# Normalization at the end of a fused convolution kernel: scale and shift in one ScalarE operation, max and sum on VectorE, and the parts in another order

## The chip, the core and the metric

The kernel runs on one core of a Trainium2 chip. A core has TensorE (PE in the profile) for matrix products, VectorE (DVE) and GpSimd (POOL) for elementwise work, ScalarE (ACT) for activations, and SyncE (SP), which here only issues transfers. Each engine works through its own instructions in order and waits for others by semaphores. Transfers run on sixteen DMA engines, whichever engine issued them. On-chip memory (SBUF) has 128 partitions; the profile writes a tile as partitions x elements.

The metric is the device time of one execution in microseconds (us), median over runs, lower is better. One further execution is taken by the hardware profiler; its instruction times, counted from the start of its span, are what the views of the profile show.

## The reference, cut to what matters

Four layers follow one another on x of 8 images, 128 channels, 64 x 64 pixels, all in float32. The change concerns only the end of the fourth and the residual sum that follows each layer: the fourth layer samples its input at learned offsets, convolves, normalizes each channel over all images and pixels, applies a leaky ReLU, and is added to the layer's input.

```python
out = jnp.einsum('bckhw,ock->bohw', samp, dcn_w.reshape(COUT, C, KK))
out = out + dcn_b[None, :, None, None]
mu = out.mean(axis=(0, 2, 3), keepdims=True)
var = out.var(axis=(0, 2, 3), keepdims=True)
out = (out - mu) * lax.rsqrt(var + 1e-05)
out = out * gamma[None, :, None, None] + beta[None, :, None, None]
return jnp.where(out >= 0, out, 0.1 * out)
```

The kernel's output is x3 plus this result, where x3 is what the first three layers have left. The mean and variance need every image, so nothing can be normalized before the last convolution is done.

## The kernel before, in words

`conv_preact_kernel` (line 35) runs layer 0, then layers 1 to 3 interleaved by a hand-made schedule, and at its very end calls `finish` (lines 1280 to 1323), which holds the whole change. Channels lie on the 128 partitions.

While layer 3 runs, `Layer3.store` (line 1266) takes the statistics of each block of 512 pixels into `st` and writes the convolution's output of the first six images to the DRAM tensor `od`. For the last two images, `KEEP = 2`, the outputs stay in SBUF (`o_kept`), and `Layer2.keep` (line 1131) has fetched the matching pieces of x3 into SBUF too (`x3k`). These are 16 small parts of 128x512: two images of eight blocks. The six other images are 24 large parts of 128x1024 (`E = 2 * T`), whose x3 and `od` pieces must be loaded. They go through `room`, the SBUF tensor X that layer 3 has used as its buffer for gathered samples. It holds eight large parts (`AHEAD = 8`), each a pair of 512 KB pieces.

`finish` works like this. SP issues the loads of the first eight large parts (line 1299), each as soon as layer 3 has left that piece of X. DVE aggregates the statistics (line 1304) and, with ACT's square root (line 1306), makes the per-channel factor `sc` (lines 1307 and 1308). Then one loop runs over the 40 parts: first the 16 small ones, then the 24 large ones. Its iteration n starts part n and ends part n - 1:

- for part n, DVE subtracts the mean and multiplies by `sc` (line 1315), and ACT adds beta (line 1316);
- for part n - 1, DVE takes the max of v and 0.1 v (line 1319), GpSimd adds v to x3 (line 1320), and ACT issues the store of the sum (line 1321). After a large part, SP issues the loads of the large part eight further on, into the same place.

This text order is the order in each engine's queue. So ACT's queue reads: activation of part n, store of part n - 1, activation of part n + 1. A store's issue waits for the sum that it stores, and what stands behind it in ACT's queue waits with it. SP's queue holds only the loads, in order; a load of x3 waits for the store that frees its place to land, and the following load of `od` stands behind it. The small parts have no loads in this stage.

Of the kernel before, what the change touches and what calls it, by code (L numbers as in the profile page):

```python
# [10 lines left out]
F32 = mybir.dt.float32  # L11
I32 = mybir.dt.int32
AF = mybir.ActivationFunctionType
ALU = mybir.AluOpType
# [3 lines left out]
P = 128  # L18
# [5 lines left out]
T = 512  # L24
# [10 lines left out]
def conv_preact_kernel(ctx: ExitStack, tc: tile.TileContext, a: dict, out: bass.AP):  # L35
# [46 lines left out]
    with tc.tile_pool(name="l2w", bufs=1) as wp, tc.tile_pool(name="l2", bufs=2) as w2, tc.tile_pool(  # L82
# [64 lines left out]
        while three.late:  # L147
            three.tick()
        finish(tc, a, eps, od, x3d, y_out, st, const, kept, three.kept, X.rearrange("p n b -> p (n b)"))


# [1128 lines left out]
def finish(tc, a, eps, od, x3d, y_out, st, wp, x3k, odk, room):  # L1280

    nc = tc.nc
    E, AHEAD = 2 * T, 8
    gamma = wp.tile([P, 1], F32, name="gamma")
    nc.sync.dma_start(gamma, a["gamma"])
    beta = wp.tile([P, 1], F32, name="beta")
    nc.sync.dma_start(beta, a["beta"])
    todo = [(b, g) for b in range(B) if (b, 0) not in odk for g in range(HW // E)]

    def place(n):  # L1290

        at = n % AHEAD * 2 * E
        return room[:, at : at + E], room[:, at + E : at + 2 * E]

    def loads(n):
        if n < len(todo):
            b, g = todo[n]
            for t, d in zip(place(n), (x3d, od)):
                nc.sync.dma_start(t, d[b][:, g * E : (g + 1) * E])

    for n in range(AHEAD):
        loads(n)
    mv = wp.tile([P, 2], F32, name="bn_mv")
    nc.vector.bn_aggr(mv, st.rearrange("p a s -> p (a s)"))
    sc = wp.tile([P, 1], F32, name="bn_sc")
    nc.scalar.activation(sc, mv[:, 1:2], AF.Sqrt, bias=eps)
    nc.vector.reciprocal(sc, sc)
    nc.vector.tensor_mul(sc, sc, gamma)

    parts = [(x3k[b, g], odk[b, g], y_out[b][:, g * T : (g + 1) * T]) for b, g in odk]  # L1310
    parts += [(*place(n), y_out[b][:, g * E : (g + 1) * E]) for n, (b, g) in enumerate(todo)]
    for n in range(len(parts) + 1):
        if n < len(parts):
            _, v, _ = parts[n]
            nc.vector.tensor_scalar(v, v, mv[:, 0:1], sc, ALU.subtract, ALU.mult)
            nc.scalar.activation(v, v, AF.Identity, bias=beta)
        if n:
            x3, v, out = parts[n - 1]
            nc.vector.scalar_tensor_tensor(v, v, 0.1, v, ALU.mult, ALU.max)
            nc.gpsimd.tensor_add(x3, x3, v)  # L1320
            nc.scalar.dma_start(out, x3)
            if n > len(odk):
                loads(n - 1 - len(odk) + AHEAD)


def layouts(i):
# [55 lines left out]
```

## Time and profile before

The runs took 7391.58, 7405.77 and 7413.39 us, median 7405.77.

| what | value |
|---|---|
| profiled execution, its own time | 7432.59 us |
| its span, first to last instruction | 7430.9 us |
| busy over the span: PE, DVE, ACT, POOL | 76%, 65%, 45%, 55% |
| factor `sc` ready, first operation of the loop (line 1315) | 7292.56 us |
| last sum on POOL (line 1320) ends | 7423.65 us |
| DVE max, 128x1024 (line 1319), 24 times | 3279 ns mean |
| DVE max, 128x512, 16 times | 1478 ns mean |
| DVE scale and subtract (line 1315), 128x1024 and 128x512 | 801 and 536 ns mean |
| ACT add beta (line 1316), 128x1024 and 128x512 | 1149 and 721 ns mean |
| POOL sum (line 1320), 128x1024 and 128x512 | 2785 and 1528 ns mean |

The engines' shares are means over the whole span, in which other stages have other limits; the stage of `finish` is read from its own stretch. In the order of time a line gives the start, the length, the engine, the source line, the operation with output and inputs, and in brackets how long the engine sat idle before it and what ended that. In the view of stretches the columns are the stretch, its length, busy time with the number of instructions of PE, PEld (weight loads), DVE, ACT and POOL, the granted TensorE clock, the mean busy share of the DMA engines, and GB/s. In the view of waits a line gives who waited for whom, the us in total, how many times, and the longest.

### The profile page before, as it was taken

How to read it: one execution, taken by the hardware profiler on the slowest of the kernel's cores; microseconds unless marked ns; L12 is line 12 of the kernel's file. 1: busy time of each engine (PE TensorE's matmuls, PEld its weight loads, DVE VectorE, ACT ScalarE, POOL GpSimd, SP SyncE). 2: the span in 40 equal slices, each digit the busy share in tenths (PEclk: the TensorE clock that was granted, in tenths of full speed). 3: DMA queues.
4: the chain of work that ended last, by engine and by line, in shares of the span. 5: the costliest groups of instructions: out<-in, count | busy, mean ns of one | idle time of the engine just before them, and what ended most of it. 6: DMA issues, size and time to landing. Idle time of an engine off the chain costs nothing.

```text
span 7430.9 us, 79727 instructions
## 1 busy us (share of the span) xinstructions
PE 5644.5 (76%) x25130; PEld 3377.1 (45%) x25130; DVE 4854.7 (65%) x6350; ACT 3346.5 (45%) x7618; POOL 4120.3 (55%) x3781
## 2 busy tenths in 40 slices
PE   6888888899999999779898988984646555565431
PEld 1222222255556556647777767762333333333220
DVE  4988889666666666230366666758767676676668
ACT  3555655433333332020255555554556555655553
POOL 4878778545545454000255555555666666666665
PEclk9888888799999999989999999996768777776665
DMA  1111111101100100130356656667666666666666
GB/s 57 43 58 54 57 56 53 42 29 34 32 30 30 31 20 18 55 128 24 98 176 194 185 183 180 193 184 246 209 214 214 210 207 207 207 204 220 181 181 245
DMA packets 358982, 926.70 MB, mean 125 GB/s; under 512 B 64040, under 2 KB 99120, under 8 KB 356512
## 3 DMA queue, kind: packets, MB, share of 16 engines
q0 software_dynamic: 184320, 604.13, 26.7%
q1 hardware_dynamic: 168480, 300.70, 12.5%
q10 hardware_dynamic: 5760, 16.78, 0.6%
q8 instruction: 200, 3.28, 0.2%
q14 instruction: 222, 1.82, 0.1%
HBM read 800.16 MB, written 121.21 MB: 124 GB/s over the span
## 4 chain that ended last, share of the span: by engine, by line
PE 55%; ACT 13%; issue 9%; DVE 8%; another core or an unknown queue 8%; POOL 4%; DMA 3%; SPq 0%; DVEq 0%; POOLq 0%; ACTq 0%
PE u_ps L743 13%; PE ps_l L743 11%; ACT X L1203 7%; PE u_ps L579 5%; PE ps_o L1246 4%; PE ps_c L488 3%; PE ps_t L904 3%; PE ps_y L633 3%; PE ps_s L1228 2%; PE ps_x L396 2%; DVE hb L614 2%; PE ps_off L1021 2%; POOL hb L625 2%; PE ps_t L930 1%
## 5 line engine op out<-in xcount | busy, mean ns | idle before, releaser
L1192 POOL DMA_INDIRECT X<-table,idx x1386 | 1315.0, 949 | 743.0 <-issue 277.7
L1192 POOL DMA_INDIRECT got<-table,idx x918 | 881.8, 961 | 1294.0 <-DVE idx L1082 528.8
L625 POOL TENSOR_TENSOR hb<-hb,bc 128x1024 f32<-128x1024 f32 x512 | 1206.2, 2356 | 47.1 <-POOL carry L620 4.5
L614 DVE TENSOR_TENSOR_SCAN hb<-da,carry,u_ps 128x512 f32<-128x512 f32 x896 | 1098.1, 1267 | 76.3 <-PE ps_y L633 19.8
L596 ACT ACTIVATE da<-dt_ps 128x1024 f32<-128x1024 f32 x512 | 524.4, 1024 | 1284.7 <-PE dt_ps L579 1088.0
L1246 PE MATMUL ps_o<-samp,dcn_w 128*128 128x256 f32 x2304 | 716.9, 458 | 221.6 <-issue 90.0
L1203 ACT ACTIVATE X<-X,wgt 128x128 f32<-128x128 f32 x2772 | 865.6, 397 | 24.4 <-issue 24.2
L1238 ACT COPY samp<-ps_s 128x384 f32<-128x384 f32 x768 | 362.6, 472 | 1056.9 <-remote 595.5
L579 PE MATMUL u_ps<-u,m_u 32*128 32x512 f32 x2048 | 653.2, 717 | 130.9 <-DVE hb L614 130.3
L603 DVE TENSOR_TENSOR u_ps<-u_ps,bc 128x1024 f32<-128x1024 f32 x512 | 625.9, 1223 | 191.2 <-PE dt_ps L579 173.9
L1228 PE MATMUL ps_s<-ident,X 128*128 128x128 f32 x1386 | 310.7, 347 | 568.5 <-ACT samp L1238 274.3
L579 PE MATMUL dt_ps<-dt,m_dt 32*128 32x512 f32 x2048 | 665.1, 729 | 31.5 <-ACT da L596 25.7
L1246 PEld LDWEIGHTS ps_o<-samp,dcn_w 128*128 128x128 f32 x2304 | 510.3, 233 | 348.8 <-issue 121.0
L1219 DVE TENSOR_TENSOR prod<-prod,X 128x384 f32<-128x384 f32 x462 | 260.8, 565 | 491.4 <-ACT X L1203 308.9
L751 DVE SCALAR_TENSOR_TENSOR X<-ps_l,X 128x256 f32<-128x256 f32 x252 | 106.7, 423 | 727.0 <-PE ps_l L743 514.1
L1203 ACT ACTIVATE got<-got,wgt 128x128 f32<-128x128 f32 x1836 | 570.3, 393 | 0.7 <-issue 0.7
L1228 PEld LDWEIGHTS ps_s<-ident,X 128*128 128x128 f32 x1386 | 208.6, 178 | 704.1 <-ACT samp L1238 336.1
L620 POOL COPY carry<-hb 128x2 f32<-128x2 f32 x512 | 110.6, 216 | 735.8 <-DVE hb L614 686.5
L1208 DVE TENSOR_TENSOR prod<-X,prod 128x768 f32<-128x768 f32 x462 | 444.3, 962 | 57.4 <-ACT prod L1175 38.3
L751 DVE SCALAR_TENSOR_TENSOR X<-u_ps,X 128x256 f32<-128x256 f32 x252 | 107.0, 425 | 562.9 <-PE u_ps L743 560.5
L904 PE MATMUL ps_t<-xn,w 128*128 128x512 f32 (+4 forms) x688 | 346.1, 658 | 69.7 <-issue 28.0
L579 PEld LDWEIGHTS u_ps<-u,m_u 32*128 32x128 f32 x2048 | 169.8, 202 | 483.8 <-DVE hb L614 281.6
(233 smaller groups left out, 10687.3 us busy)
## 6 DMA issues: line engine op xcount, KB each, us to landing
bc<-bcd SPq DMA_DIRECT2D x512, 64.0 KB
table<-tok SPq DMA_DIRECT2D x128, 256.0 KB
x<-x1d SPq DMA_DIRECT2D x96, 256.0 KB
X<-table,idx POOLq DMA_INDIRECT x1386
x<-x2d SPq DMA_DIRECT2D x48, 384.0 KB
x3h<-x3d SPq DMA_DIRECT2D x16, 1056.0 KB
x_st<-in_x SPq DMA_DIRECT2D x64, 256.0 KB
x_o<-in_x SPq DMA_DIRECT2D x64, 256.0 KB
```

The costliest lines, as they stand in the source:

```text
L579: nc.tensor.matmul(ps[:, j, :], lhsT=mask[q, r].rearrange("p d n -> p (d n)"), rhs=S[c][src, h][q, :], start=True, stop=True,)
L596: nc.scalar.activation(da, steps[i]["dt"], AF.Exp)
L603: nc.vector.tensor_mul(st["bc"], st["bc"], s["bc", h][:, 0].unsqueeze(1).to_broadcast([P, 2, T]))
L614: nc.vector.tensor_tensor_scan(hb[:, j, :], st["da"][:, j, :], st["bc"][:, j, :], start, ALU.mult, ALU.add)
L625: nc.gpsimd.tensor_mul(hb, hb, S[c]["bc", h][:, 1].unsqueeze(1).to_broadcast([P, 2, T]))
L743: nc.tensor.matmul(ps[:, c0:c1, :], lhsT=w[:, k, :], rhs=v[:, prev, c0 + k - PAD : c1 + k - PAD, :], start=(k == PAD), stop=(k == K - 1),)
L904: nc.tensor.matmul(ps[:, o0 - a0 : o1 - a0, :], lhsT=self.w1[:, k, :], rhs=S["xn", g][:, i0 + o0 : i0 + o1, :], start=(k == 2), stop=(k == 4),
L1192: nc.gpsimd.indirect_dma_start(out=got[:, k, :, :].rearrange("p q c -> p (q c)"), out_offset=None, in_=tab, in_offset=bass.IndirectOffsetO ...
L1203: nc.scalar.activation(got[:, k, q, :], got[:, k, q, :], AF.Identity, scale=wgt[:, t, k0 + k, q : q + 1])
L1208: nc.vector.tensor_mul(prod, got[:, :, 0:2, :], w.unsqueeze(3).to_broadcast([P, G3, 2, C]))
L1228: nc.tensor.transpose(ps[:, k, :], got[:, k, 0, :], self.ident)
L1246: nc.tensor.matmul(ps, lhsT=self.dcn_w[:, k, :], rhs=samp[:, k - k0, :], start=(k == 0), stop=(k == KK - 1))
```

## The change

The shift is folded: the kernel makes, once, a per-channel `bn_shift` = beta - mean x sc from two small DVE operations. With it ACT does scale and shift in one activation per part, reading the untouched v, and DVE's operation of line 1315 is gone. DVE does the max as before and then also the sum with x3; GpSimd does nothing in this stage. And the order of the parts is another one: three large parts, two small ones, and so on, eight times, where before all small parts came first. The reload of a large part still follows that part's predecessor in its place; only the counter is kept differently. SP's instructions and their order are the same as before.

```diff
     nc.vector.reciprocal(sc, sc)
     nc.vector.tensor_mul(sc, sc, gamma)
 
-    parts = [(x3k[b, g], odk[b, g], y_out[b][:, g * T : (g + 1) * T]) for b, g in odk]
-    parts += [(*place(n), y_out[b][:, g * E : (g + 1) * E]) for n, (b, g) in enumerate(todo)]
+    shift = wp.tile([P, 1], F32, name="bn_shift")
+    nc.vector.scalar_tensor_tensor(shift, mv[:, 0:1], sc, beta, ALU.mult, ALU.subtract)
+    nc.vector.tensor_scalar_mul(shift, shift, -1.0)
+
+    here = [(x3k[b, g], odk[b, g], y_out[b][:, g * T : (g + 1) * T]) for b, g in odk]
+    parts = []
+    for n, (b, g) in enumerate(todo):
+        parts.append((*place(n), y_out[b][:, g * E : (g + 1) * E]))
+        if n % 3 == 2:
+            parts += [here.pop(0) for _ in range(2) if here]
+    parts += here
+    m = AHEAD
     for n in range(len(parts) + 1):
         if n < len(parts):
             _, v, _ = parts[n]
-            nc.vector.tensor_scalar(v, v, mv[:, 0:1], sc, ALU.subtract, ALU.mult)
-            nc.scalar.activation(v, v, AF.Identity, bias=beta)
+            nc.scalar.activation(v, v, AF.Identity, bias=shift, scale=sc)
         if n:
             x3, v, out = parts[n - 1]
             nc.vector.scalar_tensor_tensor(v, v, 0.1, v, ALU.mult, ALU.max)
-            nc.gpsimd.tensor_add(x3, x3, v)
+            nc.vector.tensor_add(x3, x3, v)
             nc.scalar.dma_start(out, x3)
-            if n > len(odk):
-                loads(n - 1 - len(odk) + AHEAD)
+            if x3.shape[-1] == E:
+                loads(m)
+                m += 1
```

## The prediction

> **What bounds the kernel now.** I read three views of the profiled execution: the stretches of the end stage, then its order of time, then its waits. The change lies wholly behind the last convolution, so only the last 139 us of 7430.9 count.
>
> The first view is busy time by stretch: length, busy us of PE, PEld, DVE, ACT and POOL with instruction counts, granted clock, DMA share, GB/s.
>
> ```profile
> 7300.00:7324.00 24.00, 0.00 (x0) 0.00 (x0) 22.18 (x23) 7.94 (x11) 16.90 (x12) 0.50 0.32 121
> 7324.00:7340.00 16.00, 0.00 (x0) 0.00 (x0) 15.68 (x11) 5.32 (x5) 11.29 (x5) 0.50 0.43 148
> 7340.00:7356.00 16.00, 0.00 (x0) 0.00 (x0) 16.00 (x9) 4.59 (x4) 11.19 (x5) 0.50 0.86 297
> 7356.00:7402.00 46.00, 0.00 (x0) 0.00 (x0) 46.00 (x24) 13.58 (x12) 32.05 (x13) 0.50 1.01 395
> ```
>
> DVE looks full all along. The DMA engines do little for the first 40 us, while the sixteen small parts go through, and are full (395 GB/s) only later. Is DVE's fullness work? The order of time (start, length, engine, line) answers:
>
> ```profile
> 7293.90 0.69 DVE L1319 SCALAR_TENSOR_TENSOR o_kept<-o_kept 128x512 f32<-128x512 f32 x1 [0.33 <-ACT o_kept L1316]
> ...
> 7361.62 0.80 DVE L1315 TENSOR_SCALAR X<-X,bn_mv,bn_sc 128x1024 f32<-128x1024 f32 x1
> 7361.78 2.84 POOL L1320 TENSOR_TENSOR X<-X 128x1024 f32<-128x1024 f32 x1 [1.16 <-DVE X L1319]
> 7362.35 3.36 DVE L1319 SCALAR_TENSOR_TENSOR X<-X 128x1024 f32<-128x1024 f32 x1
> ...
> 7365.62 0.80 DVE L1315 TENSOR_SCALAR X<-X,bn_mv,bn_sc 128x1024 f32<-128x1024 f32 x1
> ```
>
> The first max (512 elements), with GpSimd still idle, took 0.69. A later one of 1024 took 3.36: GpSimd's add ends at 7361.78 + 2.84 = 7364.62 and the max at 7362.35 + 3.36 = 7365.71, only 1.09 later. So the max stood still until the add was over. The add in turn lasts 2.84 here but 2.34 in the last part, where no L1315 runs beside it. DVE and GpSimd take turns: 2.34 add, 1.1 max, some 0.5 scale-and-subtract. The period from L1315 to L1315 is 7365.62 - 7361.62 = 4.00 for a large part; for a small one the starts stand 2.13 apart. Sum 24 x 4.00 + 16 x 2.13 = 130.1; in the trace, from 7292.56 to the last add's end at 7423.65, it is 131.1. The waits show who is held:
>
> ```profile
> ACT X L1316 <- POOL X L1320: 62.8, 22, 2.9
> POOL X L1320 <- DVE X L1319: 25.8, 22, 1.2
> ACT o_kept L1316 <- POOL x3k L1320: 20.4, 14, 2.1
> ```
>
> ACT waits for the adds, since the store's issue (L1321) stands in its queue; DVE hardly waits for anybody on record.
>
> **What the Trainium skill says.** "SBUF — State Buffer", section "Who interferes with whom": a DVE instruction with two SBUF inputs, or in a 2-port mode, and a GpSimd one share a port pair as an exclusive lock, and the second blocks fully. The 1.09 above agrees. "VectorE: DVE Perf Modes", section on the TRN2 errata: an fp32 add of two tensors takes (N+151)/0.96 ns, so 0.69 for 512 and 1.22 for 1024. The trace agrees at 512: 0.686 at L949, an add with one input from PSUM. "ScalarE: Activation LUTs", section "What ACT_TABLE_LOAD costs": each pointer operand of an activation adds about 93 ns. No row here has dense data and two pointers. "DMA: Bandwidth & Descriptors", section "Issuing engines are not separate DMA queues": transfers from ACT and SP share the same 16 engines; the 1.01 share while both queues work agrees.
>
> **The change, part by part.** All times below are those of the profiled execution.
>
> Setup: bn_shift costs two 128x1 DVE operations; L768 shows 0.22 and L1308 0.16 for such, some 0.45 with gaps. The 0.54 of L1315 ahead of the first activation goes. First activation near 7293.1, as before (7293.14). Worth zero within 0.3.
>
> L1315 goes (24 x 0.80, 16 x 0.54), and the activation takes scale as a second pointer: 1.15 + 0.09 = 1.24 large, 0.72 + 0.09 = 0.81 small (estimate from the page). From below it costs nothing more. From above, L721, the only row with both pointers, takes 1.305 for 512, but its output is strided over four batches; I don't take it. Cover: ACT then has 24 x 1.24 + 16 x 0.81 = 42.7, plus 40 issues at 0.34 (13.5), against 83 on DVE.
>
> GpSimd's adds go to DVE, and the lock goes. DVE per large part: max 1.22 + add 1.22 + two gaps of 0.03 (L947 starts 0.78 after L945, which lasts 0.75) = 2.50. The max at 1024 is 0.69 plus 512/0.96 ns. Small: 0.69 + 0.69 + 0.06 = 1.44. Sum 24 x 2.50 + 16 x 1.44 = 83.0, against 130.1.
>
> ACT's queue is ordered activation n, store n-1, activation n+1. The store's issue waits for add n-1; behind it stands activation n+1, and max n+1 waits for that. From the end of add n-1: 0.38 issue with semaphores + 1.24 = 1.62, while DVE does part n, 2.50 or 1.44. Only where n is a second small part and a large one follows does DVE wait, some 0.2, seven times: 1.5.
>
> Interleaving: three large, two small, eight times. Nothing moves on SP's queue; each reload (two transfers of 0.524 MB) still waits for the store of its buffer, eight large parts back. But it is asked for earlier: the first large store goes out near 7297, not 7332.6. Traffic behind 7297: 16 reloads x 1.049 = 16.8 MB and stores 24 x 0.524 + 16 x 0.262 = 16.8 MB, 33.6 in all. DVE alone would ask for 5.24 MB (3 x 0.524 + 2 x 0.262 stored, 3 x 1.049 loaded) in each 3 x 2.50 + 2 x 1.44 = 10.4 us: 504 GB/s, over the 395 of the full stretch (its full slices show 410 and more). So once the eight parts in hand are used up, **transfers set the pace**: they are what is late next.
>
> The sum: the initial loads end near 7297 (in the trace the rate falls to 121 GB/s by 7300), so the flow starts at 7298. When the last load lands, all but some 1.6 MB of stores has moved: 32.0 MB / 0.395 = 81.0, so 7379, and with about 1 for the landing 7380. Then the last large part, 1.2 + 2.5, and two small ones, 2.9: 7386.6. From the last add's end to the span's end it was 7430.9 - 7423.65 = 7.25; with a store of half the size (0.65 less at 395 GB/s) 6.6. Span 7393.2: **38 us less**. At 410 GB/s it is 41 less. Below 395, 2 KB rows of the small stores may cost: their 0.32 share at 121 GB/s means 378 when full, which on 4.2 MB adds 0.5.
>
> The profiled execution took 7432.6, 27 above the median of the runs (7405.8, runs 7391.6 to 7413.4); the end stage is not where I can see that, so I take the 38 off the median: **7368 us**.
>
> **The rivals.** *Vector alone sets the pace* (transfers keep up): first max 7294.4 + 83.0 + 1.5 + 6.6 = 7385.5, 45 less, 7361. For it: 8 parts in hand at the start. Against: 504 GB/s asked, where the highest slice of the transfers' view (7340 to 7402) has 423.
>
> *Transfers come slower than 395*, since reloads wait for stores and a store's issue can stand behind an activation waiting for a load: at 340 GB/s the last load lands at 7393, span 7406.5, 24 less, 7381. For it: stores under full traffic took up to 9.9 us from issue to the reload (7344.64 to 7354.49), and 7340 to 7356 ran at 297 with DVE never idle. Against: there, reloads had only begun.
>
> *Slower: the ring of eight buffers starves.* One round trip (store, reload, compute) would have to exceed 8 x 5.2 us, which is (7423.65 - 7298)/24 per large part; then break-even is 32.0 MB in some 118 us, 270 GB/s, and a clear loss (22 us) needs 228. At 225 the last load lands near 7441: span 7454, 23 more, 7429. For it: the stretch before the end ran at 191 GB/s (7240 to 7270), but on gathers. Against: 46 us at 395 in the same ring.
>
> *The max stays slow without GpSimd*, so the change doesn't do what it says: 24 x (3.36 + 1.25) + 16 x 2.2 = 146, 16 more, 7422. The 0.69 at 7293.90 speaks against it.
>
> **How the numbers follow.** The forecast (gain 34 to 43) has 0.80, vector alone 0.05, slower transfers 0.10, the starving ring 0.03, the slow max 0.02. What a measurement can tell from no change is about 0.3%, 22 us. The forecast's own range is 7363 to 7372, widened by the scatter of a median (runs lie 22 apart) to 7352 to 7384. With vector alone's 7361 less scatter, and slower transfers' 7381 with some, the range is 7347 to 7388. Faster: 0.80 + 0.05, less a little for scatter, plus half of slower transfers, 0.87; within 0.3%: the rest of these and the slow max, 0.10; slower 0.03.
>
> **What would show it.** Right: from the first max on, 1.22 and 0.69 for max and add; no POOL busy in the end stage; DVE full until some 30 to 50 us in, then idle time put down to ACT's activations, and those waiting for loads; DMA share near 1 from about 7300 to 7380; last large part's activation close behind the last load. Wrong: DMA share well under 0.9 with DVE idle (the ring), activations over 2 us, or a max that keeps 3 us.

## The result, and the profile after

The changed kernel takes 7360.31 us (median of 6 runs, 7352.98 to 7377.2), the kernel before 7401.13 us in the same comparison (6 runs, 7391.58 to 7413.39). The ratio is 0.9947 with a 95% interval of 0.9933 to 0.9962: 28 to 50 us less, by the medians 40.8.

The profiled executions differ by more, 7430.9 - 7375.5 = 55.4 us of span, and not all of it is owed to the change. I cut both spans at the same two places: where `sc` is ready (line 1308), and where the last sum ends. I call the stretch between them the loop and what follows it the tail.

| | before | after | difference |
|---|---|---|---|
| ahead of the loop | 7292.5 | 7272.3 | 20.2 |
| loop, 40 parts | 131.1 | 100.1 | 31.0 |
| tail | 7.25 | 3.1 | 4.15 |
| span | 7430.9 | 7375.5 | 55.4 |

The code ahead of the loop is the same in both, and over the experiments below this start lies anywhere from 7249.2 to 7300.2 without order. The runs of one kernel lie 22 us (before) and 24 us (after) apart too. So I put the 20.2 down to scatter from one execution to the next; the stage of `finish` gained 35.2. Below I compare loops and tails, each from one trace, and give for whole kernels the measured ratio to the kernel before with its 95% interval; it differs slightly from the quotient of the medians.

The costliest groups of the stage, as line, engine, operation, output and inputs, count | busy us, mean ns of one | idle us just before them, and what ended it. First the large max of before, then the groups after the change:

```profile
L1319 DVE SCALAR_TENSOR_TENSOR X<-X 128x1024 f32<-128x1024 f32 x24 | 78.7, 3279 | 0.8 <-ACT X L1316 0.8
```

```profile
L1327 ACT ACTIVATE X<-X,bn_shift,bn_sc 128x1024 f32<-128x1024 f32 x24 | 29.5, 1239 | 37.2 <-DMA X<-od 22.8 <-DVE X L1331 6.7 <-DVE x3k L1331 3.2
L1331 DVE TENSOR_TENSOR X<-X 128x1024 f32<-128x1024 f32 x24 | 29.4, 1224 | 0.8
L1330 DVE SCALAR_TENSOR_TENSOR X<-X 128x1024 f32<-128x1024 f32 x24 | 29.3, 1221 | 19.7 <-ACT X L1327 19.7
L1327 ACT ACTIVATE o_kept<-o_kept,bn_shift,bn_sc 128x512 f32<-128x512 f32 x16 | 12.9, 809 | 19.8 <-DVE X L1331 19.8
L1331 DVE TENSOR_TENSOR x3k<-x3k,o_kept 128x512 f32<-128x512 f32 x16 | 11.1, 692 | 0.5
L1330 DVE SCALAR_TENSOR_TENSOR o_kept<-o_kept 128x512 f32<-128x512 f32 x16 | 11.0, 688 | 0.0
```

The large max fell from 3279 to 1221 ns, the small one from 1478 to 688. The sum on DVE costs 1224 and 692 ns, the folded activation 1239 and 809. Every single operation is as fast as was worked out. But DVE stands idle 19.7 us ahead of large parts, always for ACT; and ACT in turn loses 22.8 us to a load of `od`. The waits (who waited for whom: us in total, times, longest):

```profile
ACT X L1327 <- DMA X<-od: 22.8, 4, 6.3
...
ACT o_kept L1327 <- DVE X L1331: 19.8, 12, 2.2
DVE X L1330 <- ACT X L1327: 19.7, 12, 4.6
```

Four waits make the 22.8, each of 4.8 to 6.3 us. An activation of a large part does need its load of `od`, so this looks like transfers that are too slow. The order of time says otherwise. Below, the two loads of the twelfth large part; then the load of `od` for the fifteenth, the tenth part's sum, its store, and the twelfth's activation with the max that waited for it; at the end an undisturbed run of large parts:

```profile
7294.37 0.32 SPq L1299 DMA_DIRECT2D X<-x3d  x1
...
7294.74 0.43 SPq L1299 DMA_DIRECT2D X<-od  x1
...
7309.50 0.43 SPq L1299 DMA_DIRECT2D X<-od  x1
...
7310.17 1.22 DVE L1331 TENSOR_TENSOR X<-X 128x1024 f32<-128x1024 f32 x1
...
7316.70 0.34 ACTq L1332 DMA_DIRECT2D out<-X  x1
7317.09 1.24 ACT L1327 ACTIVATE X<-X,bn_shift,bn_sc 128x1024 f32<-128x1024 f32 x1 [6.30 <-DMA X<-od]
...
7318.36 1.23 DVE L1330 SCALAR_TENSOR_TENSOR X<-X 128x1024 f32<-128x1024 f32 x1 [4.58 <-ACT X L1327]
...
7354.57 1.22 DVE L1330 SCALAR_TENSOR_TENSOR X<-X 128x1024 f32<-128x1024 f32 x1
...
7355.82 1.22 DVE L1331 TENSOR_TENSOR X<-X 128x1024 f32<-128x1024 f32 x1
...
7356.96 1.22 DVE L1330 SCALAR_TENSOR_TENSOR X<-X 128x1024 f32<-128x1024 f32 x1
```

The twelfth part's own loads were issued at 7294.37 and 7294.74, 22 us ahead of its activation. The sum to be stored was ready at 7310.17 + 1.22 = 7311.39, yet its store went out only at 7316.70, 5.31 later; the activation stands behind that store in ACT's queue and starts 0.39 after it. So what was held is the store. In the list of instructions of the built program, transfers issued by SP and ACT announce their ends on eight semaphores that they take in turn; those of GpSimd have eight others. The store of the tenth part uses the semaphore that the load of `od` for the fifteenth part used, eight transfers earlier, and therefore waits for that load, which has nothing to do with it. A large part has three transfers and a small one has one, so eight are fewer than three large parts' worth. The same stall falls in four of the eight cycles of three large and two small parts, the third to the sixth: activations at 7302.14, 7317.09, 7331.11 and 7345.39 waited 4.80, 6.30, 5.92 and 5.78 us. Each belongs to a part whose own loads were issued some 22 us before, and by the list of instructions the store ahead of each waits for the load of `od` three large parts further on. That load had been issued 6.7 to 7.2 us before the store went out.

The stretches after (length, busy us of PE, PEld, DVE, ACT and POOL with counts, granted clock, DMA share, GB/s):

```profile
7290.00:7300.00 10.00, 0.00 (x0) 0.00 (x0) 7.94 (x10) 3.69 (x4) 0.00 (x0) 0.50 1.03 409
...
7310.00:7320.00 10.00, 0.00 (x0) 0.00 (x0) 5.32 (x6) 2.73 (x3) 0.00 (x0) 0.50 0.99 378
7320.00:7330.00 10.00, 0.00 (x0) 0.00 (x0) 8.27 (x9) 3.29 (x3) 0.00 (x0) 0.50 0.94 337
...
7340.00:7350.00 10.00, 0.00 (x0) 0.00 (x0) 6.00 (x7) 2.38 (x3) 0.00 (x0) 0.50 0.99 382
7350.00:7360.00 10.00, 0.00 (x0) 0.00 (x0) 9.53 (x10) 5.06 (x6) 0.00 (x0) 0.50 0.95 361
7360.00:7365.00 5.00, 0.00 (x0) 0.00 (x0) 4.56 (x7) 3.15 (x3) 0.00 (x0) 0.50 0.56 220
```

DVE works only 5.3 or 6.0 of 10 us where a stall falls, and the DMA engines still show a share of 0.94 to 1.03. Read alone, the share says "transfers set the pace". But the bytes say 337 to 382 GB/s, below the 409 of the first line. From 7360 on the transfers are half idle, and DVE is full to the end: 12 us in which arithmetic that is left over sets the end.

### The profile page after: what moved, and what is told of

Read it like the earlier page. It is cut to its first block, busy times and chain, and to the rows that moved or that the text cites. A ratio compares the mean times of both kernels' runs of the same rounds, so it can differ in the third digit from the quotient of the medians.

```text
span 7375.5 us, 79658 instructions
## 1 busy us (share of the span) xinstructions
PE 5651.5 (77%) x25130; PEld 3386.2 (46%) x25130; DVE 4807.7 (65%) x6352; ACT 3354.5 (45%) x7618; POOL 4028.7 (55%) x3741
## 4 chain that ended last, share of the span: by engine, by line
PE 56%; ACT 12%; DVE 10%; issue 9%; another core or an unknown queue 7%; DMA 3%; POOL 2%; SPq 0%; DVEq 0%; ACTq 0%; POOLq 0%
PE u_ps L743 13%; PE ps_l L743 11%; ACT X L1203 7%; PE u_ps L579 5%; PE ps_o L1246 5%; PE ps_c L488 3%; PE ps_t L904 3%; DVE hb L614 3%; PE ps_y L633 3%; PE ps_x L396 2%; PE ps_s L1228 2%; PE ps_off L1021 2%; DVE u_ps L603 2%; PE ps_t L930 1%
## 5 line engine op out<-in xcount | busy, mean ns | idle before, releaser
L614 DVE TENSOR_TENSOR_SCAN hb<-da,carry,u_ps 128x512 f32<-128x512 f32 x896 | 1097.8, 1267 | 76.6 <-PE ps_y L633 19.2
L1208 DVE TENSOR_TENSOR prod<-X,prod 128x768 f32<-128x768 f32 x462 | 444.4, 962 | 33.3 <-ACT prod L1175 14.4
```

The costliest lines, as they stand in the source:

```text
L614: nc.vector.tensor_tensor_scan(hb[:, j, :], st["da"][:, j, :], st["bc"][:, j, :], start, ALU.mult, ALU.add)
L1208: nc.vector.tensor_mul(prod, got[:, :, 0:2, :], w.unsqueeze(3).to_broadcast([P, G3, 2, C]))
```

## The experiments

Two theories stood against each other for the 100.1 us. One: the bytes (33.6 MB) set the pace, and the stalls only show it. The other: the stalls are a cost of their own, from a store held for an unrelated load in front of an activation. Beside them stood the question which of the change's three parts brought the gain. All kernels keep the changed kernel's order of parts unless it is said.

### Which part of the change brought it

**Order alone.** The operations of before, in the new order of parts:

```diff
-            nc.scalar.activation(v, v, AF.Identity, bias=shift, scale=sc)
+            nc.vector.tensor_scalar(v, v, mv[:, 0:1], sc, ALU.subtract, ALU.mult)
+            nc.scalar.activation(v, v, AF.Identity, bias=beta)
...
-            nc.vector.tensor_add(x3, x3, v)
+            nc.gpsimd.tensor_add(x3, x3, v)
```

(the two operations for `bn_shift` go as well)

> The operations of the kernel before in the interleaved order. The loop is counted from the end of the operation that makes the factor (line 1308) to the end of the last sum: 131.1 us before, 100.1 after. If VectorE and GpSimd taking turns set the pace, the order is worth nothing alone: 24 x 4.00 + 16 x 2.13 = 130, a loop of 129 to 132 and the time of before. If starting the reloads earlier is a gain of its own, the loop is under 125.

Measured: loop 131.4, tail 7.22; 7403.83 us beside 7395.94 of before, ratio 1.0007 (0.9998 to 1.0016). Where DVE and GpSimd take turns over 4 us per large part, it is worth nothing that transfers may start earlier.

**Operations alone.** The new operations, but the small parts first as before:

```diff
-    here = [(x3k[b, g], odk[b, g], y_out[b][:, g * T : (g + 1) * T]) for b, g in odk]
-    parts = []
-    for n, (b, g) in enumerate(todo):
-        parts.append((*place(n), y_out[b][:, g * E : (g + 1) * E]))
-        if n % 3 == 2:
-            parts += [here.pop(0) for _ in range(2) if here]
-    parts += here
+    parts = [(x3k[b, g], odk[b, g], y_out[b][:, g * T : (g + 1) * T]) for b, g in odk]
+    parts += [(*place(n), y_out[b][:, g * E : (g + 1) * E]) for n, (b, g) in enumerate(todo)]
```

> The new operations in the old order, small parts first. If transfers set the pace after the change: small parts 16 x 1.35 = 22 us with stores alone, then 29.4 MB at 390 GB/s = 75 us, and some 8 us of start and end: a loop of 103 to 108, so 3 to 8 us longer than with the interleaved order. If VectorE's own work sets it, 24 x 2.39 + 16 x 1.35 = 79 and a loop of 81 to 84 in either order. If the stalls come from how stores and loads wait for each other and not from bytes, the loop stays near 100.

Measured: loop 101.5, tail 3.71; ratio 0.9943 (0.9923 to 0.9964). That is the result of the whole change but for 1.4 us of loop and 0.6 of tail, in one trace each. So the order of the parts has brought next to nothing in this change. My forecast had put it on the path: without it transfers would start late and the loop be longer.

But the nearly equal loops have different limits. Two of this kernel's stretches:

```profile
7320.00:7330.00 10.00, 0.00 (x0) 0.00 (x0) 3.88 (x5) 3.61 (x3) 0.00 (x0) 0.50 1.03 420
7350.00:7360.00 10.00, 0.00 (x0) 0.00 (x0) 6.73 (x6) 2.48 (x2) 0.00 (x0) 0.50 1.03 417
```

From 7320 to 7360 its transfers ran at 417 to 420 GB/s while DVE worked 3.9 to 8.2 of 10 us: here bytes that start late do set the pace. The expectation's 29.4 MB take 70 us at 420 GB/s and not 75, which lowers its 103 to 108 to 98 to 103. Stalls like those of the change are not needed for that; by the list of instructions only 4 of this kernel's 40 stores wait for a reload, against 18 in the change, since eight transfers back mostly stands another store.

**Sum on GpSimd.** The changed kernel, with the sum left where it was:

```diff
-            nc.vector.tensor_add(x3, x3, v)
+            nc.gpsimd.tensor_add(x3, x3, v)
```

> As after, but GpSimd makes the sum again. If the two engines lock each other out, max and sum never overlap: 2.34 + 1.12 = 3.46 for a large part, about 2.05 for a small one, a loop near 116, and max records of 2 to 3 us. If there is no lock and GpSimd only keeps its own pace, 24 x 2.34 + 16 x 1.43 = 79, hidden by transfers: a loop near 100 and max records of 1.22. From the last sum to the end of the span it was 7.25 before and 3.1 after: 6 to 7 here if GpSimd having worked last is what lengthens the end, 3 to 4 if not.

Measured: loop 116.5, tail 7.22; ratio 0.9975 (0.9964 to 0.9987). The groups of this kernel:

```profile
L1331 POOL TENSOR_TENSOR X<-X 128x1024 f32<-128x1024 f32 x24 | 57.4, 2392 | 57.6 <-DVE X L1330 55.3 <-DMA out<-x3k 1.2 <-DMA X<-od 1.2
L1330 DVE SCALAR_TENSOR_TENSOR X<-X 128x1024 f32<-128x1024 f32 x24 | 50.6, 2112 | 25.4 <-ACT X L1327 25.4
```

and two lines of its order of time:

```profile
7299.89 2.34 POOL L1331 TENSOR_TENSOR X<-X 128x1024 f32<-128x1024 f32 x1 [1.16 <-DVE X L1330]
...
7300.42 2.89 DVE L1330 SCALAR_TENSOR_TENSOR X<-X 128x1024 f32<-128x1024 f32 x1 [0.61 <-ACT X L1327]
```

The sum ends at 7302.23 and the max at 7303.31, 1.08 later, though it had started 1.81 before the sum's end. The same max on the same data takes 1221 ns where DVE makes the sum. This agrees with the exclusive lock that the page "SBUF — State Buffer" of the Trainium skill describes (section "Who interferes with whom"), and the delay is gone when the sum, and nothing else, is taken off GpSimd.

**Sum alone.** The changed kernel with scale and subtract on DVE again (one execution only):

```diff
-            nc.scalar.activation(v, v, AF.Identity, bias=shift, scale=sc)
+            nc.vector.tensor_scalar(v, v, mv[:, 0:1], sc, ALU.subtract, ALU.mult)
+            nc.scalar.activation(v, v, AF.Identity, bias=beta)
```

> As after, but VectorE still subtracts the mean and scales (0.80 and 0.54) and ScalarE only adds beta; the sum is on VectorE. VectorE's own work is then 24 x (2.39 + 0.75) + 16 x (1.35 + 0.50) = 105: a loop of 105 to 108 if VectorE sets the pace, so that folding the scale into ScalarE's operation is worth 5 to 8 us of the whole. If transfers hide it, 100 to 102 and the folding is worth nothing here.

Measured: loop 111.0, tail 3.10, 3 to 6 us above what was expected. DVE is idle less than after the change, but the expectation had counted no idle time, and its max waited for ACT for 6.5 us in all, about the excess:

```profile
DVE X L1331 <- ACT X L1328: 6.5, 6, 1.7
```

With the others this makes a square, all in the new order of parts:

| loop, us | sum on GpSimd | sum on DVE |
|---|---|---|
| scale and subtract on DVE | 131.4 | 111.0 |
| folded into the activation | 116.5 | 100.1 |

Moving the sum is worth 20.4 or 16.4, folding 14.9 or 10.9. The two operations of line 1315 took 19.2 + 8.5 = 27.7 us of DVE in the profile of before, so folding returns much less than it takes away: what DVE saves in work, it partly waits for ACT.

### What costs the rest

**No reloads.** The call `loads(m)` in the loop is left out, so the 16 large parts after the first eight are computed from what lies in their place: the output lacks their data, and half of the stage's bytes are gone.

```diff
-                loads(m)
                 m += 1
```

> As after, but the 16 reloads are left out: large parts 9 to 24 work on whatever lies in their place, so 16.8 MB are not moved. If transfers hold VectorE up, its work alone remains: 24 x 2.39 + 16 x 1.35 = 79, plus 1.3 for the first activation and some 2 for the queue order on ScalarE: a loop of 81 to 84. If the order of activations and stores on ScalarE is what holds it, the loop stays above 95.

Measured: loop 83.8, tail 3.04; ratio 0.9933 (0.9917 to 0.9950). DVE's idle time is almost gone, in the group of the large max:

```profile
L1330 DVE SCALAR_TENSOR_TENSOR X<-X 128x1024 f32<-128x1024 f32 x24 | 29.3, 1220 | 3.7 <-ACT X L1327 3.7
```

So DVE and ACT, with the first loads and the stores alone, need 83.8, and the reloads bring 16.3 more: by their bytes, or by the stalls. The next three kernels tell these apart, each moving the same bytes as the change.

**Stores issued by GpSimd.** A held store no longer stands in ACT's queue, and it takes its semaphore from the other eight:

```diff
-            nc.scalar.dma_start(out, x3)
+            nc.gpsimd.dma_start(out, x3)
```

> As after, but GpSimd issues the stores. All transfers that SP and ScalarE issue take eight completion semaphores in turn, so a transfer waits for the one eight issues before it, a store for an unrelated load too; GpSimd's transfers have eight of their own. In after the order alone gained nothing over small parts first (100.1 and 101.5). If stores held behind unrelated loads, and activations behind those stores, make the 17 us by which the loop exceeds the 83.8 without reloads, then only bytes remain: 33.6 MB at 390 to 410 GB/s from some 5 us into the loop, and 5 us of end: a loop of 90 to 95. If it is bytes alone that come late, the loop stays at 99 to 102. If issuing on GpSimd costs more than it saves, it is longer.

Measured: loop 91.9, tail 3.91; ratio 0.9936 (0.9919 to 0.9954). Its waits:

```profile
ACT X L1327 <- DMA X<-od: 47.4, 16, 4.0
...
DVE X L1330 <- ACT X L1327: 12.1, 7, 2.5
```

No store stands in ACT's queue here, so ACT runs ahead and these waits are for its own data; of 47.4 us only 12.1 reach DVE.

**Reloads issued by GpSimd.** The stores stay in ACT's queue, but share their semaphores with loads no more:

```diff
-                nc.sync.dma_start(t, d[b][:, g * E : (g + 1) * E])
+                (nc.sync if n < AHEAD else nc.gpsimd).dma_start(t, d[b][:, g * E : (g + 1) * E])
```

> As after, but GpSimd issues the 16 reloads and ScalarE keeps the stores; stores then share semaphores with stores alone, and stay in ScalarE's queue between the activations. If the shared semaphores are the cause, the loop is 90 to 95 here too. If the stores' place in ScalarE's queue is the cause by itself, it stays at 98 or more here and only the run with stores on GpSimd is short. If bytes alone are the cause, both stay at 99 to 102.

Measured: loop 91.5, tail 3.04; ratio 0.9939 (0.9923 to 0.9956). The order of ACT's queue is the changed kernel's, and the stalls near 6 us are gone; what is left is 3.5 at most, in this kernel's waits:

```profile
ACT X L1327 <- DMA X<-od: 14.5, 5, 3.5
DVE X L1330 <- ACT X L1327: 10.9, 13, 2.3
```

In its stretches the same bytes now go faster, at the same share:

```profile
7300.00:7310.00 10.00, 0.00 (x0) 0.00 (x0) 9.49 (x11) 5.35 (x5) 3.14 (x6) 0.50 1.03 413
7310.00:7320.00 10.00, 0.00 (x0) 0.00 (x0) 9.49 (x11) 5.34 (x5) 3.14 (x6) 0.50 1.03 417
```

DVE works 9.5 us of 10 in these stretches. From 7330 to 7360 it falls to 8.7, 8.4 and 7.3 at 418 to 419 GB/s: with the stalls gone, the transfers themselves become what is late.

In both kernels with GpSimd issuing, loads too are held less. In the change the load of `od` for the seventeenth part went out 3.85 us after that of x3 (7311.54 and 7315.39), since it waits for the fifteenth part's load of x3. The next kernel leaves the sharing as it is.

**Store one part later.** SP and ACT share their semaphores as in the change, but ACT issues each store one part later, so that one more activation is ahead of it:

```diff
             nc.vector.tensor_add(x3, x3, v)
-            nc.scalar.dma_start(out, x3)
+        for k in [n - 2] * (n > 1) + [n - 1] * (n == len(parts)):
+            x3, _, out = parts[k]
+            nc.scalar.dma_start(out, x3)
```

(with the reload behind it in the same inner loop, so it too is issued one part later)

> As after, but ScalarE issues each store (and SP the reload that follows it) one part later, so that the sum is done long before and an activation stands behind a store that should be ready; the semaphores are shared as before. If shared semaphores hold the stores, the activations still stand behind them: a loop of 98 to 102. If only the order of activation and store on ScalarE costs, the loop is 90 to 96. If bytes alone set it, 99 to 103.

Measured: loop 90.2, tail 3.05; ratio 0.9938 (0.9920 to 0.9955). This falsified the form of my theory in which sharing the semaphores is the cost by itself. The holds are still there (20 of its 40 stores wait for a reload, 18 in the change), as its waits show:

```profile
ACT X L1327 <- DMA X<-x3d: 17.2, 5, 4.6
...
DVE X L1330 <- ACT X L1327: 9.0, 4, 3.0
...
ACT o_kept L1327 <- DMA X<-x3d: 5.5, 3, 3.7
```

A hold is not for the activation's own data: an activation reads no x3, and in the last line a small part (`o_kept`) loads nothing in this stage at all. But ACT loses 17.2 + 5.5 us to holds, and DVE only 9.0, where it was 22.8 and 19.7 after the change: with one part more in hand, a hold on ACT no longer reaches DVE whole. So the loss of about 9 us needs both: a store held for an unrelated load, and the next activation close behind it with nothing in hand. Each of the three cures breaks one of the two, or both.

**Store later, reloads by GpSimd.** Both cures together:

> Both cures: each store one part later, and the reloads issued by GpSimd with semaphores of their own. If bytes set what is left (33.6 MB at 390 to 410 GB/s and some 7 us around them), the loop stays at 88 to 91, as with one cure. If stalls are still in the 90.2, it comes near the 83.8 of the kernel without reloads: 84 to 87. Against the kernel before: 44 to 51 us less.

Measured: loop 90.8, tail 3.13; ratio 0.9935 (0.9918 to 0.9952). They don't add up, since each alone already removes the same loss. What stays above the 83.8 without reloads, some 7 us, I put down to bytes that come late: DVE's waits for ACT are 11.0 us here and ACT's for loads of `od` 25.9, and the transfers ran at 417 to 419 GB/s from 7300 to 7360. No run isolates this remainder.

**Store later, small parts first.** The late store with the order of before:

> Each store one part later, and the small parts first as in the kernel before. With the stalls in place the two orders gave 100.1 and 101.5. If the interleaved order is worth something once the stalls are short, because the transfers have work from the start, the loop is 97 to 102 here against 90.2 interleaved: 22 us of small parts with stores alone, then 29.4 MB at 390 to 400 GB/s. If the order has no worth of its own, about 90.

Measured: loop 99.5, tail 3.72; ratio 0.9958 (0.9941 to 0.9976). Its waits:

```profile
ACT X L1322 <- DMA X<-od: 27.1, 10, 3.8
...
DVE X L1325 <- ACT X L1322: 18.1, 14, 2.5
```

With the late store, the new order is worth 99.5 - 90.2 = 9.3 us of loop; with the store as in the change 101.5 - 100.1 = 1.4. So interleaving does what was forecast, transfers start early and work under the small parts, and the stalls of the change take it back.

**GpSimd early, DVE at the end.** Is the shorter tail due to GpSimd's absence from the stage, or from its end? GpSimd makes the first 35 sums and DVE the last five (one execution only):

```diff
-            nc.vector.tensor_add(x3, x3, v)
+            (nc.gpsimd if n <= 35 else nc.vector).tensor_add(x3, x3, v)
```

> GpSimd makes the first 35 sums and VectorE the last five. From the last sum to the end of the span it was 7.2 in the three kernels in which GpSimd made the last sum, and 3.0 to 3.7 in the three in which VectorE did. If the end waits for GpSimd because it worked last, 3 to 4 here; if any sum of GpSimd in this stage lengthens the end, 7. The loop: 116.5 with all sums on GpSimd, less three large parts at 1.07 and two small ones at 0.7 each, so about 112.

Measured: loop 111.7, tail 3.10. The tail is short as soon as GpSimd isn't the last to compute, here by five parts.

No version is clearly better than the change by its ratio: the three cures and the pair lie at 0.9935 to 0.9939, the change at 0.9947, the intervals overlap, and they were not all measured on one chip. The loops of these four are 8.2 to 9.9 us shorter in the trace, 0.1% of the kernel. I recommend none of them over the others; moving the stores or the reloads to GpSimd is a change of one line.

## Why the prediction was right, and where it was not

Forecast 7368 us, 38 less than before, range 7347 to 7388; measured 7360.31, 40.8 less by the medians, and the profiled spans' share of the stage is 35.2. Time and sign are right. The sum behind them was right in its work and wrong in how the stage ends: the loop was 6.0 us too short in it and the tail 3.5 too long, and that these cancelled in part was luck.

- **Setup at zero**: right. The first activation starts 0.48 after `sc` is ready (7272.75 - 7272.27), before 0.62 (7293.14 - 7292.52); the two operations for `bn_shift` take 0.22 and 0.15.
- **L1315 goes, the activation costs 1.24 and 0.81**: measured 1239 and 809 ns. The second pointer operand costs 90 and 88 ns against 1149 and 721 before; "ScalarE: Activation LUTs" of the Trainium skill (section "What ACT_TABLE_LOAD costs") states about 93.
- **The sum goes to DVE and the lock goes**: right. 1224 and 692 ns for the sums agree with the (N + 151)/0.96 ns that "VectorE: DVE Perf Modes" of the Trainium skill gives for an fp32 add (section on the TRN2 errata; 1224 and 691). The max took about as long, 1221 and 688. DVE per large part was predicted at 2.50 and is 7356.96 - 7354.57 = 2.39, per small part 1.44 and 1.35: 24 x 2.39 + 16 x 1.35 = 79.0 in place of 83.0. The predicted gaps of 0.03 hold for only one of the two: the sum starts 0.03 after the max's recorded end, and the next max 0.08 before the sum's.
- **ACT's queue costs DVE 1.5 in all**: wrong, and it is the origin of the miss in the loop. I looked at the store's wait for the sum alone, and took its issue as free once the sum was ready. DVE waited 19.7 us for ACT in all, 14.4 of them in the four stalls behind held stores (2.29 + 4.58 + 3.64 + 3.90).
- **Transfers set the pace at 395 GB/s, the last load lands 87.5 us into the loop**: half right. From the end of the load queue it landed about 86.7 us in. But the mean rate from 7290 to 7360 was 378 GB/s (409, 395, 378, 337, 381, 382 and 361 in its stretches of 10 us). The load was nevertheless in time, partly since the stores were further behind than forecast: those of four large and four small parts, 4 x 0.524 + 4 x 0.262 = 3.1 MB, had not even been issued, against 1.6 MB. Where the stalls are gone the forecast's limit does appear: the transfers of the four kernels with a cure ran at 400 to 421 GB/s in their full stretches (share 1.03), and their loops took 90.2 to 91.9 us, against the 94.1 worked out with 395.
- **Then one large and two small parts, 6.6 us to the last sum**: this is the step that failed. When the last load had landed, the sums of three large and four small parts were still to be made: 3 x 2.39 + 4 x 1.35 = 12.6 of DVE, and with a wait the last sum came 13.4 later, at 100.1 instead of 94.1. DVE had lost its lead in the stalls, so its own rest set the end, not the last load. The other account gives the same: 79.0 of work and 19.7 of idle time are 98.7; the 1.4 left are the two small operations for `bn_shift`, 0.4, and gaps that the undisturbed parts don't show.
- **Tail 6.6**: wrong, 3.1. I took the 7.25 of before for the landing of the last store and scaled it by size. It was GpSimd's own end. The 3.5 too much here hid 3.5 of the 6.0 too little there; 6.0 - 3.5 = 2.5 is what parts the forecast's 37.7 from the 35.2 of the trace.

Of the rivals, "vector alone" (45 less) fell: DVE idled 19.7 us. "Slower transfers" (24 less) named a store's issue behind an activation that waits for a load. What happened was the reverse, an activation behind a store held for a load; and the rate was not the limit, nor was there a loss of that size. The starving ring and the slow max did not come: the large max took 1221 ns. The sign I had for "right", idle DVE put down to activations and these to loads, did appear and would have passed for a confirmation. Another sign stayed out: the last large part's activation was to come close behind the last load, and came 6.4 us after it (7365.36, against 7359.0). It was the issue times, and then the kernels with the same bytes in 90 to 92 us, that showed otherwise.

## What to carry to other kernels

When a wait is put down to a load, compare it with the time at which that operand's own load was issued; if that is long past, look at what stands ahead in the same queue, and ask which unrelated transfer it may be held for. A store in a computing engine's queue is not only an issue of 0.34 us: give it one part of slack, or let transfers of another kind go through another set of semaphores. And cost a tail by what ends last in it, here an engine's own end, before scaling it with bytes.

## What the runs showed of the hardware that I had not expected

**The program's end waits for GpSimd if it computed last.** From the last sum to the end of the span it is 7.25 us before, 7.22 in each of the two other kernels in which GpSimd makes the last sum, and 3.0 to 3.9 in all that have it on DVE, 3.10 also where GpSimd makes the first 35. GpSimd's drain in the view of the last source line (shortest, median and longest in ns, first to last start), first of before, then of the kernel with only the sum on GpSimd:

```profile
L1379 POOLq DRAIN  x3: 40/102/8835, 7421.3 to 7430.6; - x3
```

```profile
L1391 POOLq DRAIN  x3: 40/102/7757, 7366.0 to 7374.3; - x3
```

Before, the longest began at 7421.3, when the last sum started, and ended at 7430.1, 6.5 us after that sum; the last transfer was over by 7426. In the other it is 7366.0 + 7.76 = 7373.8, again 6.5 after the last sum's end (7367.3). Where GpSimd makes the first 35 sums, its longest drain takes 7.77 us too, but from 7381.9 on, and so is over 3.3 us ahead of the last sum's end on DVE (7393.0).

**A DMA share near 1 is not a rate.** 378 GB/s at a share of 0.99 after the change and 417 at 1.03 with the reloads on GpSimd move the same kinds of transfers. Why the share stays high at the lower rate was not settled.
